# A two-block MetaFormer kernel: order of work in the outlook stage, and smaller portions of side work in attention

## The chip, the cores and the metric

The kernel runs on one core of one Trainium2 chip. The metric is the device time of one execution in microseconds (us). The core has five engines that run their own instruction streams: TensorE (PE) for matrix products, VectorE (DVE), ScalarE (ACT), GpSimd (POOL) and SyncE (SP), which here only issues DMA transfers. Engines wait for one another by semaphores. Everything is computed in fp32.

## The reference

The input x has 4 images of 32 x 32 positions (1024 tokens each) and 384 channels. Two blocks follow one another, each with a mixing part and a feed-forward part, and each part is added to its input.

```python
# block 0, mixing: attention with grouped queries
q, k, v = heads(qkv_w @ ln_c(x))                      # 12 heads of 32, N = 1024 tokens
attn = softmax(q k^T * scale)
gw = one_hot(argmax(q gp^T))                          # each query's group, 48 groups a head
q_mean = mean of the q of a group;  qmw = q_mean k^T  # (48 groups, N)
mask = the 96 largest of each row of qmw
attn = attn * row * mask.sum(groups);  attn /= attn.sum(over queries) + 1e-8
x = x + (attn v) @ proj_w^T
# block 0, feed-forward: 4 experts of width 1536, the best 2 of each token, gelu
x = x + sum_e weight_e * (gelu(ln_t(x) w1_e) w2_e)
# block 1, mixing: outlook attention, 3 x 3 windows, 12 heads
v = ln_c(x) Wv^T;  a = ln_c(x) Wa^T                   # a: 12 heads x 9 x 9 at each position
attn = softmax(a * scale, last axis)
out = attn @ (v of the 9 neighbours);  y = the 9 outputs added back onto the 9 neighbours
x = x + y @ Wo^T
# block 1, feed-forward with Kronecker weights
h = gelu(ln_t(x) kron(c_fc_1, c_fc_2)^T);  x = x + h kron(c_proj_1, c_proj_2)^T
```

## The kernel before

Tokens lie in 32 tiles of 128 (8 tiles an image). The kernel runs four stages in one program: attention (`attention`, line 159), experts (`experts`, 1547), outlook (`outlook`, 1767), and the Kronecker feed-forward (`Kron.run`, 2173). Attention and outlook are under a manual schedule: every engine's instructions stand in the order in which the Python code emits them. So an instruction that waits holds back all that its engine was given after it. The same is true of the DMA issues of SyncE.

**Attention.** The main loop takes 192 steps of some 5.7 us, 4 a head, 12 heads an image, 4 images. In a step u of head n it emits the scores of a pair of key tiles (L627, TensorE), their exponentials (L637, ScalarE), the product with v of an earlier step (L645 into ps_o) and the row sums (L645 into ps_z). In step u == 0 of the next head, `gather` copies the sums and sends them over two small DMAs (z_row L661, zz L663). In u == 1 `spread` adds them, inverts them and sends them out again (r_row L675, rz L677), so that rz holds one value a query on all partitions. `share` (L689, VectorE) multiplies the exponentials with rz, and with the mask's count. A `Head` object, when made, issues eight DMAs that copy q and k of its head into q4 and k4; it is made at u == 1 of the head before, at the very end of the step.

Beside this main work each step carries side work for other heads and images, written as Python generators that are advanced once or a few times a step: `prepare` (normalise, turn, q and k of an image), `groups` (the one-hot groups and the group means; `choose` and `tally` are its two later parts), `topk` (an iterative search for the 96th value of each row; `search` advances it twice a step), and `routed`, `Router.route`, `Router.first` and `Router.schedule` (the routing of tokens to experts, advanced once a step). `prepare` and `groups` yield a price and a condition; `prepared` takes the next portion if its condition holds, until a step's budget (PACE) is spent. `topk` and the routing yield only to end a portion. `later(f)` runs f at the beginning of the next step; `ends` holds what is emitted when the main work and the portions of a step are.

In `topk`, a VectorE chain (L377 to L407) ends with the value `between`; then comes a yield, and then the ScalarE instruction L411, which counts what lies above it. ScalarE has the next exponentials behind it.

**Outlook.** A loop over steps i = 0 to 31 and a few more. Step i makes, for tile i: the scores (`scores`, twelve matmuls ps_a L1881, with a maximum and a subtraction on VectorE, L1887 and L1888), the exponentials (`exps`, L1895, ScalarE), the normalised next tile (`norm`, xn L147), its transposition (`turn`, ps_tr L155, ScalarE copy L156), `values` (ps_v L1928) and `share`: VectorE adds up the nine exponentials of a window (L1901 to L1905, tiles a_rows and a_sum), inverts (L1906), multiplies (L1908), and SyncE issues the moves of the normalised shares by one row of the image (L1918, L1919 into up; L1920, L1922 into down; about 40 to 122 KB each).

For the tile two steps back: `outer` (two ScalarE copies, L1942 and L1943, of the moved shares into u; they stand ahead of the exponentials of tile i on ScalarE), `inner` (three VectorE additions, L1949 to L1951) and `band`: six matmuls ps_c L1960, two multiplications into co (L1968), a DMA of co into a DRAM buffer (room, L1975, 150 KB), and, when that has landed, a DMA that reads it back as a band (L1981, 1560 KB); SyncE itself waits for the landing of room before it issues the read. For the tile four steps back: `sort` (three ScalarE copies L1991 of the landed band into own) and `gather` (ps_y L2004, the product with v). Finished rows go through `mix` (ps_wo L2019) and `mixed` (added to x, L2026). `add` brings in the experts' output for later tiles (yt, L1541 and L1844).

Loads for later tiles are issued in steps 1, 2, 5 and 8; step 8 has `Kron.load`, which issues the weights of the last stage and then emits on VectorE the sums that need them (f2sum L2127, row, wide).

Of the kernel before, what the change touches and what calls it, by code (L numbers as in the profile page):

```python
# [10 lines left out]
FP = mybir.dt.float32  # L11
# [6 lines left out]
P = 128  # L18
# [140 lines left out]
def attention(net, outer, router, x, x1, unsafe, qkv_wT, gpT, proj_wT, proj_w, gate_w, gate_b):  # L159
# [24 lines left out]
    with ExitStack() as ctx:  # L184
# [161 lines left out]
        def topk(b, t):  # L346
# [61 lines left out]
            yield  # L408
            over = small("tk_over")
# [40 lines left out]
        def prepare(b):  # L450
# [22 lines left out]
            for half in range(2):  # L473
# [6 lines left out]
                for t in range(4):  # L480
                    st = tiny.tile([P, 6], FP, name="ln_st", tag="ln_st", bufs=2)
                    nc.vector.bn_stats(st, xt[:, t, :])
                    nc.vector.bn_aggr(mv[:, t, :], st)
                    if t % 2:
                        yield 0.3, None
# [45 lines left out]
        def groups(b):  # L531

            im = images[b]
            for c in range(KC):
# [28 lines left out]
                def tally(two, ones_):  # L563
                    one = NB // 2 * (KC * b + c) + two
                    nc.scalar.activation(ones_, ones_, AF.Copy, accum_out=onehot[:, one : one + 1])
                    chosen.append(two)
# [204 lines left out]
        def routed(b):  # L771
# [25 lines left out]
            if b == B - 2:  # L797
                yield
                router.first()
# [63 lines left out]
        for step in range(STEPS + OUT + 2):  # L863
# [42 lines left out]
            if u == 1 and n + 1 < NHEAD:  # L906
                heads.append(Head(n + 1))
# [307 lines left out]
class Router:  # L1215
# [71 lines left out]
    def route(self, b, logit, mean, rs):  # L1287
# [20 lines left out]
        nc.vector.tensor_tensor(prob, prob, all_(one), ALU.mult)  # L1308
        pairs = [P, NB, NE, NE]
# [3 lines left out]
        for t, op, mask in ((ge, ALU.is_ge, self.lower), (gt, ALU.is_gt, self.upper)):  # L1313
            nc.vector.tensor_tensor(t, other, mine, op)
            nc.vector.tensor_tensor(t, t, mask.unsqueeze(1).to_broadcast(pairs), ALU.mult)
        nc.vector.tensor_tensor(ge, ge, gt, ALU.add)
# [28 lines left out]
        nc.vector.tensor_tensor(at, src, base.unsqueeze(1).to_broadcast(wide), ALU.add)  # L1345

# [8 lines left out]
        nc.vector.tensor_reduce(slot[1], part, AX.X, ALU.max)  # L1355
        there = []
# [25 lines left out]
    def first(self):  # L1382
# [9 lines left out]
        nc.vector.tensor_reduce(full, fills, AX.X, ALU.add)  # L1392

# [12 lines left out]
        nc.vector.tensor_scalar(pre, pre, float(NFIRST), float(UNITS), ALU.min, ALU.mult)  # L1406
        self.firsts = self.rows(self.pool, "first", NFIRST, 1)
# [359 lines left out]
def outlook(net, wv, wa, wo, left, router, kron, loads):  # L1767
# [15 lines left out]
    with ExitStack() as ctx:  # L1783
# [113 lines left out]
        def share(i):  # L1897
            b, t = place(i)
# [4 lines left out]
            sm = work.tile([P, 2, PW], FP, name="a_sum", tag="a_sum")  # L1903
            nc.vector.tensor_tensor(sm, rows[:, :, 0, :], rows[:, :, 1, :], ALU.add)
            nc.vector.tensor_tensor(sm, sm, rows[:, :, 2, :], ALU.add)  # L1905
            nc.vector.reciprocal(sm, sm)  # L1906
# [132 lines left out]
        for step in range(last + 1):  # L2039
# [5 lines left out]
            if 0 <= i - 2 < NT:  # L2045
                outer(i - 2)
            if i < NT:
                scores(i, 0)
                scores(i, 1)
                exps(i)  # L2050
            if 0 <= i - 2 < NT:
                inner(i - 2)
            if i + 1 < NT:
                xn = norm(i + 1)
            done = []
            for one in mixes.pop(step, []):
                done.append(mix(*one))
                if len(done) == 2:
                    mixed(*done[0])
                    mixed(*done[1])  # L2060
                    gauged += [j for j, _ in done]
                    done = []
            if 0 <= i - LAG < NT:
                gather(i - LAG, 0 if (i - LAG) % NB < 5 else 1)
            if i + 1 < NT:
                turn(i + 1, xn)
            for one in done:
                mixed(*one)
                gauged.append(one[0])
# [3 lines left out]
            if 0 <= i - 2 < NT:  # L2073
                band(i - 2)
# [22 lines left out]
class Kron:  # L2097
# [19 lines left out]
    def load(self, fc1T, fc2, proj1T, proj2):  # L2117
# [7 lines left out]
        nc.sync.dma_start(out=p2, in_=proj2.rearrange("a b -> (a b)").partition_broadcast(P))  # L2125
        self.f2sum = const.tile([P, 1], FP, name="f2sum")
# [166 lines left out]
def metaformer_kernel(  # L2293
# [19 lines left out]
    def rest(router, done):  # L2313

        with ExitStack() as late:
# [17 lines left out]
            def weigh(queue, tile_, w):  # L2333
# [9 lines left out]
                8: lambda: kron.load(fc1T, fc2, proj1T, proj2),  # L2343
            }
# [14 lines left out]
    with tc.If(tc.nc.values_load(unsafe[0:1, 0:1], min_val=0, max_val=1) != 0):  # L2359
        with ExitStack() as outer:  # L2360
# [4 lines left out]
            with ExitStack() as inner:  # L2365
                router = routing(inner)
                for b, given in enumerate(gates(net, router.psum, gate_w, gate_b)):
                    for _ in router.route(b, *given):
                        pass
                    if b == B - 2:  # L2370
                        router.first()
# [61 lines left out]
```

## Time and profile before

| what | value |
|---|---|
| time, median of 3 runs | 2778.15 us (2777.52 to 2788.7) |
| profiled execution | 2777.38 us, its span 2774.9 us |
| TensorE busy | 2565.5 us, 92% of the span, mean granted clock 0.959 |

The stages, in us of the span (with the busy time of TensorE, VectorE and ScalarE in each window):

| stage | window | length | PE | DVE | ACT | granted clock |
|---|---|---|---|---|---|---|
| loading, first preparing | 0 to 80 | 80 | 54.32 | 14.27 | 30.01 | 1.00 |
| attention | 80 to 1208 | 1128 | 1015.31 | 810.85 | 818.97 | 0.93 |
| experts | 1208 to 2251 | 1043 | 1029.13 | 532.03 | 202.48 | 1.00 |
| outlook | 2251 to 2686 | 435 | 388.88 | 346.24 | 197.64 | 0.95 |
| Kronecker feed-forward | 2686 to 2775 | 89 | 77.81 | 24.90 | 52.76 | 0.89 |

The scores of the outlook steps 0 to 31 start at 2251.45, 2260.84, 2270.12, 2282.46, 2295.0, 2305.85, 2316.71, 2328.42, 2343.71, 2371.64, 2383.57, 2395.25, 2408.52, 2419.85, 2431.52, 2443.19, 2454.51, 2466.89, 2478.76, 2490.44, 2503.72, 2515.04, 2526.71, 2538.38, 2549.71, 2563.80, 2575.66, 2587.34, 2600.61, 2611.93, 2623.60 and 2635.28 us.

How to read the lines further down: in a timeline, the start in us, the duration, the engine (SPq is SyncE's DMA issues), the line and operation, output <- inputs, and in brackets how long the engine sat idle before and what released it. In a table of waits: who waited, at which line, for whom; us in total, how many times, the longest. The granted clock is the share of full speed that TensorE was given.

### The profile page before, as it was taken

To read this page: it belongs to the slowest core of one execution; us is meant where nothing else is said; L and a number is where in the kernel's file an instruction comes from. 1 tells how busy PE (TensorE), PEld (TensorE's weight loads), DVE (VectorE), ACT (ScalarE), POOL (GpSimd) and SP (SyncE) were. 2 spreads that over 40 slices of the span, in tenths; PEclk is the share of its full clock that TensorE was granted. 3 is DMA by queue.
4 is the path that set the end of the run, shared out by engine and by line. 5 is a ranking of instruction groups with operands and counts; after the bars stand their busy time and mean duration, and the time that the engine had idled before them with its cause. 6 is when DMAs were issued, how large, how long until landed. Compare 5 with 4: busy or idle time off the path is not lost. (4 is left out here: it accounts for less than half of the span.)

```text
span 2774.9 us, 40133 instructions
## 1 busy us (share of the span) xinstructions
PE 2565.5 (92%) x14667; PEld 1558.3 (56%) x14667; DVE 1728.3 (62%) x4362; ACT 1301.9 (47%) x2119; POOL 417.8 (15%) x501
## 2 busy tenths in 40 slices
PE   6889999999999998789999999999999987999988
PEld 3323333333333332247889999999999953555532
DVE  1367778677778787647444544465455556887962
ACT  3778777677778777412221221121121123455455
POOL 1000000030003001413211112222222101110000
PEclk9989999999999998889999999999999999999989
DMA  5133434322322232454665545655655447565532
GB/s 108 33 103 92 108 86 126 95 60 63 96 73 64 59 107 69 133 175 160 230 238 207 202 170 216 232 194 217 237 205 211 175 145 221 165 201 175 173 110 93
DMA packets 215806, 404.13 MB, mean 146 GB/s; under 512 B 83344, under 2 KB 176848, under 8 KB 202544
## 3 DMA queue, kind: packets, MB, share of 16 engines
q1 hardware_dynamic: 184496, 187.82, 22.6%
q0 software_dynamic: 26960, 209.05, 22.0%
q10 hardware_dynamic: 4144, 4.61, 0.5%
q8 instruction: 118, 1.93, 0.3%
q14 instruction: 88, 0.72, 0.1%
HBM read 304.34 MB, written 49.00 MB: 127 GB/s over the span
## 5 line engine op out<-in xcount | busy, mean ns | idle before, releaser
L1702 ACT ACTIVATE h<-ps_h,up 128x256 f32<-128x256 f32 (+1 forms) x420 | 195.1, 465 | 825.3 <-PE ps_h L1697 823.7
L1697 PE MATMUL ps_h<-xbT,up 128*128 128x256 f32 (+1 forms) x2520 | 531.1, 371 | 2.5 <-ACT h L1702 1.8
L689 DVE CUSTOM_DVE_ANT_0 e<-e,rz,inv 128x1024 f32<-128x1024 f32 x384 | 475.3, 1274 | 47.3 <-DMA rz<-r_row 47.3
L1697 PEld LDWEIGHTS ps_h<-xbT,up 128*128 128x128 f32 x2520 | 462.6, 191 | 64.6 <-ACT h L1702 2.6
L637 ACT ACTIVATE e<-ps_s,ten 128x1024 f32<-128x1024 f32 x384 | 408.0, 1109 | 66.6 <-PE ps_s L627 40.1
L627 PE MATMUL ps_s<-q,k 32*128 32x512 f32 x1536 | 297.4, 671 | 51.5 <-ACT e L637 35.0
L645 PE MATMUL ps_o<-e,wv 128*32 128x512 f32 x1536 | 227.2, 666 | 40.3 <-DVE wv L696 38.8
L716 POOL DMA_DIRECT2D q<-po x96 | 76.2, 886 | 947.6 <-DMA q<-po 452.9
L645 PE MATMUL ps_z<-e,rt_ones 128*32 128x512 f32 x1536 | 217.1, 639 | 0.0
L373 ACT ACTIVATE below<-tk_left,tk_bound 128x1024 bf16<-128x1024 f32 (+1 forms) x160 | 184.4, 1152 | 52.4 <-DVE tk_bound L379 41.4
L1741 PE MATMUL ps_y<-wsum,hsum 128*128 128x192 f32 x1116 | 196.0, 329 | 9.5 <-DVE hsum L1657 5.2
L627 PEld LDWEIGHTS ps_s<-q,k 32*128 32x128 f32 x1536 | 92.8, 191 | 189.1 <-ACT e L637 92.0
L1741 PEld LDWEIGHTS ps_y<-wsum,hsum 128*128 128x128 f32 x1116 | 182.5, 191 | 13.2 <-DVE hsum L1657 6.6
L1881 PE MATMUL ps_a<-wa,xnT 128*128 128x486 f32 x384 | 162.1, 571 | 0.6 <-ACT xnT L156 0.6
L1745 DVE TENSOR_TENSOR y<-ps_y,y 128x192 f32<-128x192 f32 x155 | 55.5, 358 | 165.5 <-PE ps_y L1741 162.4
L645 PEld LDWEIGHTS ps_o<-e,wv 128*32 128x32 f32 x1536 | 31.5, 112 | 201.0 <-issue 66.1
L288 PE MATMUL ps_t<-xnT,wqkv 128*128 128x512 f32 x288 | 134.6, 607 | 2.4 <-ACT xnT L470 1.7
L1541 POOL DMA_INDIRECT yt<-yg,index x64 | 78.1, 1220 | 375.5 <-DVE x L1844 181.4
L645 PEld LDWEIGHTS ps_z<-e,rt_ones 128*32 128x32 f32 x1536 | 52.2, 117 | 132.0 <-issue 128.8
L1741 PE MATMUL ps_y<-down,h 128*128 128x192 f32 x744 | 126.0, 326 | 0.0
L1741 PEld LDWEIGHTS ps_y<-down,h 128*128 128x128 f32 x744 | 122.6, 190 | 1.6
L1991 ACT COPY own<-band 128x1040 f32<-128x1040 f32 x96 | 101.7, 1125 | 33.2 <-DMA band<-room 30.8
(398 smaller groups left out, 3576.7 us busy)
## 6 DMA issues: line engine op xcount, KB each, us to landing
band<-room SPq DMA_DIRECT2D x32, 1560.0 KB
rz<-r_row SPq DMA_DIRECT2D x48, 512.0 KB
yg<-y SPq DMA_DIRECT2D x67, 192.0 KB
q<-q SPq DMA_DIRECT2D x192, 64.0 KB
k<-k SPq DMA_DIRECT2D x192, 64.0 KB
room<-none SPq DMA_DIRECT2D x64, 192.0 KB
x<-x SPq DMA_DIRECT2D x35, 192.0 KB
o<-in_x_dram SPq DMA_DIRECT2D x33, 192.0 KB
```

The lines of the kernel that those rows point to most:

```text
L288: nc.tensor.matmul(ps, lhsT=lhsT(k), rhs=rhs(k), start=k == 0, stop=k == KC - 1)
L373: nc.scalar.activation(junk[:n], left[:n], AF.Sign, bias=bound[:n], accum_out=over[:n])
L627: nc.tensor.matmul(ps[:, half * 512 : half * 512 + 512], lhsT=self.k4[r, u * P : (u + 1) * P], rhs=self.q4[r, :], start=True, stop=True,)
L637: nc.scalar.activation(e, ps, AF.Exp, bias=shift, scale=QK_SCALE)
L645: nc.tensor.matmul(ps[r : r + 32, :], lhsT=lhsT(odd), rhs=self.es[2 * u + odd][:, half * 512 : half * 512 + 512], start=u == 0, stop=u == ...
L689: nc.vector.tensor_tensor_reduce(self.es[m], self.es[m], self.rz, 1.0, self.im["inv"][:, m, self.h : self.h + 1], ALU.mult, ALU.add, self. ...
L1541: self.nc.gpsimd.indirect_dma_start(out=y, out_offset=None, in_=self.net.yg[: first_row(self.complete(i // NB)), :], in_offset=bass.Indire ...
L1697: nc.tensor.matmul(ps, lhsT=up[:, o : o + P], rhs=xbT[:, k, :size], start=k == 0, stop=k == KC - 1,)
L1702: nc.scalar.activation(hs[f // 3][:, f % 3, :size], ps, AF.Gelu, bias=up[:, KC * HID + f : KC * HID + f + 1])
L1741: nc.tensor.matmul(ps, lhsT=left[f], rhs=right[:, f, :], start=f == 0, stop=f == HF - 1)
L1881: nc.tensor.matmul(pa[:, :HW_], lhsT=xnTs[i][:, k, :], rhs=wa[:, k, hh * HW_ : (hh + 1) * HW_], start=k == 0, stop=k == KC - 1,)
L1991: nc.scalar.copy(own[:, pairs], m.rearrange("p t (n h) -> p n t h", h=2)[:, pairs])
```

## The change

No arithmetic changes. In the outlook loop, `norm` of the next tile is emitted ahead of the scores. `share` is cut in two: `total` (the sums of the window) and the rest. `mixed`, then `total`, then `band` of the tile two back are emitted before `gather`, `turn`, `values` and the rest of `share`; before, `band` came after them. `Kron.load` keeps its loads at step 8, and its VectorE part moves into `Kron.fold` at step 14.

In attention, `topk` gets one more yield between the VectorE chain and L411. `prepare` for images after the first spaces its statistics by a step. `tally` marks a portion as chosen one step later, which the condition in `groups` waits for. `Router.route`, `first` and `schedule` get more yields. A `Head` is made at u == 0 of the head before, if its q and k are ready, and at u == 1 as before if not.

```diff
@@ -406,6 +406,7 @@
             nc.vector.scalar_tensor_tensor(between[:n], last[:n], -(1 - 2.0**-23), none[:n], ALU.mult, ALU.subtract)
             nc.vector.tensor_scalar(own[:n], hsel[:n, t, :], none[:n], 2.0, ALU.mult, ALU.mult)
             yield
+            yield
             over = small("tk_over")
             sign = left.bitcast(BF)[:, :NTOK]
             nc.scalar.activation(sign[:n], left[:n], AF.Sign, bias=between[:n], accum_out=over[:n])
@@ -482,7 +483,7 @@
                     nc.vector.bn_stats(st, xt[:, t, :])
                     nc.vector.bn_aggr(mv[:, t, :], st)
                     if t % 2:
-                        yield 0.3, None
+                        yield 0.3, after(1) if b else None
                 std = im["std"][:, 4 * half : 4 * half + 4]
                 nc.scalar.activation(std, mv[:, :, 1], AF.Sqrt, bias=net.eps["c"])
                 yield 0.3, after(1) if b else None
@@ -563,7 +564,7 @@
                 def tally(two, ones_):
                     one = NB // 2 * (KC * b + c) + two
                     nc.scalar.activation(ones_, ones_, AF.Copy, accum_out=onehot[:, one : one + 1])
-                    chosen.append(two)
+                    later(lambda: chosen.append(two))
 
                 for two in range(NB // 2):
                     yield 0.7, lambda: not ends
@@ -796,7 +797,7 @@
             yield from router.route(b, logit, im["mv"][:, :, 0], rs)
             if b == B - 2:
                 yield
-                router.first()
+                yield from router.first()
             if b == B - 1:
                 yield
                 yield from router.schedule(late[0])
@@ -903,7 +904,7 @@
             search()
             end()
             search()
-            if u == 1 and n + 1 < NHEAD:
+            if u < 2 and len(heads) == n + 1 < NHEAD and (u or ((n + 1) // NH, (n + 1) % NH // 4, "qk") in reached):
                 heads.append(Head(n + 1))
         residue(B - 1, 0)
         assert not ends and not others
@@ -1306,6 +1307,7 @@
         nc.vector.tensor_reduce(one, prob, AX.X, ALU.add)
         nc.vector.reciprocal(one, one)
         nc.vector.tensor_tensor(prob, prob, all_(one), ALU.mult)
+        yield
         pairs = [P, NB, NE, NE]
         ge, gt = self.temp("ge", pairs), self.temp("gt", pairs)
         other = prob.unsqueeze(2).to_broadcast(pairs)
@@ -1313,6 +1315,7 @@
         for t, op, mask in ((ge, ALU.is_ge, self.lower), (gt, ALU.is_gt, self.upper)):
             nc.vector.tensor_tensor(t, other, mine, op)
             nc.vector.tensor_tensor(t, t, mask.unsqueeze(1).to_broadcast(pairs), ALU.mult)
+        yield
         nc.vector.tensor_tensor(ge, ge, gt, ALU.add)
         sel, at = self.sel[:, tiles, :], self.at[:, tiles, :]
         nc.vector.tensor_reduce(sel, ge, AX.X, ALU.add)
@@ -1343,6 +1346,7 @@
         nc.vector.tensor_tensor(self.upto[:, b + 1, :], self.upto[:, b, :], pc[:, NE : 2 * NE], ALU.add)
         nc.vector.tensor_tensor(base, base, self.region, ALU.add)
         nc.vector.tensor_tensor(at, src, base.unsqueeze(1).to_broadcast(wide), ALU.add)
+        yield
 
         part = self.temp("part", wide)
         big = float(2 * NE * NT * P)
@@ -1353,6 +1357,7 @@
         nc.vector.tensor_scalar(slot[0], slot[0], -1.0, big, ALU.mult, ALU.add)
         nc.vector.tensor_tensor(part, at, sel, ALU.mult)
         nc.vector.tensor_reduce(slot[1], part, AX.X, ALU.max)
+        yield
         there = []
         for n in range(2):
             i = self.temp(f"there_{n}", [P, NB], mybir.dt.int32)
@@ -1390,6 +1395,7 @@
             fills, full.unsqueeze(2).to_broadcast(shape), self.steps.unsqueeze(1).to_broadcast(shape), ALU.is_ge
         )
         nc.vector.tensor_reduce(full, fills, AX.X, ALU.add)
+        yield
 
         self.start = self.pool.tile([P, B + 2, NE], FP, name="rt_start")
         self.begun = self.pool.tile([P, B + 2, NE], FP, name="rt_begun")
@@ -1404,6 +1410,7 @@
         nc.vector.tensor_tensor(taken, taken, full, ALU.min)
         nc.vector.tensor_scalar(taken, taken, float(UNITS), None, ALU.mult)
         nc.vector.tensor_scalar(pre, pre, float(NFIRST), float(UNITS), ALU.min, ALU.mult)
+        yield
         self.firsts = self.rows(self.pool, "first", NFIRST, 1)
 
     def rows(self, pool, name, n, groups):
@@ -1894,15 +1901,20 @@
             flat = attn[i].rearrange("p y s x e -> p (y s x e)")
             nc.scalar.activation(flat, flat, AF.Exp, scale=QK_SCALE)
 
-        def share(i):
-            b, t = place(i)
+        sums = {}
+
+        def total(i):
             a = attn[i]
             rows = work.tile([P, 2, 3, PW], FP, name="a_rows", tag="a_rows", bufs=1)
             nc.vector.tensor_tensor(rows, a[:, 0], a[:, 1], ALU.add)
             nc.vector.tensor_tensor(rows, rows, a[:, 2], ALU.add)
-            sm = work.tile([P, 2, PW], FP, name="a_sum", tag="a_sum")
+            sm = sums[i] = work.tile([P, 2, PW], FP, name="a_sum", tag="a_sum")
             nc.vector.tensor_tensor(sm, rows[:, :, 0, :], rows[:, :, 1, :], ALU.add)
             nc.vector.tensor_tensor(sm, sm, rows[:, :, 2, :], ALU.add)
+
+        def share(i):
+            b, t = place(i)
+            a, sm = attn[i], sums.pop(i)
             nc.vector.reciprocal(sm, sm)
             for qi in (0, 2, 1):
                 nc.vector.tensor_tensor(
@@ -2044,14 +2056,14 @@
                 sort(i - LAG)
             if 0 <= i - 2 < NT:
                 outer(i - 2)
+            if i + 1 < NT:
+                xn = norm(i + 1)
             if i < NT:
                 scores(i, 0)
                 scores(i, 1)
                 exps(i)
             if 0 <= i - 2 < NT:
                 inner(i - 2)
-            if i + 1 < NT:
-                xn = norm(i + 1)
             done = []
             for one in mixes.pop(step, []):
                 done.append(mix(*one))
@@ -2060,18 +2072,20 @@
                     mixed(*done[1])
                     gauged += [j for j, _ in done]
                     done = []
+            for one in done:
+                mixed(*one)
+                gauged.append(one[0])
+            if i < NT:
+                total(i)
+            if 0 <= i - 2 < NT:
+                band(i - 2)
             if 0 <= i - LAG < NT:
                 gather(i - LAG, 0 if (i - LAG) % NB < 5 else 1)
             if i + 1 < NT:
                 turn(i + 1, xn)
-            for one in done:
-                mixed(*one)
-                gauged.append(one[0])
             if i < NT:
                 values(i)
                 share(i)
-            if 0 <= i - 2 < NT:
-                band(i - 2)
             if 0 <= i - LAG < NT and (i - LAG) % NB == 4:
                 gather(i - LAG - 1, 1)
                 gather(i - LAG, 1)
@@ -2123,6 +2137,10 @@
         nc.sync.dma_start(out=self.wp, in_=proj1T.rearrange("(f p) a -> p f a", p=P))
         nc.sync.dma_start(out=self.f2, in_=fc2.rearrange("a b -> (a b)").partition_broadcast(P))
         nc.sync.dma_start(out=p2, in_=proj2.rearrange("a b -> (a b)").partition_broadcast(P))
+
+    def fold(self):
+        nc, A, K = self.nc, self.A, self.K
+        const, p2 = self.const, self.p2
         self.f2sum = const.tile([P, 1], FP, name="f2sum")
         nc.vector.tensor_reduce(self.f2sum, self.f2, AX.X, ALU.add)
 
@@ -2341,6 +2359,7 @@
                 2: lambda: fetch(2),
                 5: lambda: fetch(3),
                 8: lambda: kron.load(fc1T, fc2, proj1T, proj2),
+                14: kron.fold,
             }
             eng = mybir.EngineType
             with tc.manual_schedule(engines={eng.PE, eng.DVE, eng.Activation, eng.SP, eng.Pool}):
@@ -2368,7 +2387,8 @@
                     for _ in router.route(b, *given):
                         pass
                     if b == B - 2:
-                        router.first()
+                        for _ in router.first():
+                            pass
                 done = experts(net, router, x1, x2, wup, wdown, router.schedule)
         rest(router, done)
 
```

## Prediction

> **What bounds the kernel now.** I read the page's busy shares first, then time by stage, then waits inside the two stages that change, then single instructions and the chain.
>
> ```profile
> span 2774.9 us, 40133 instructions
> PE 2565.5 (92%) x14667; PEld 1558.3 (56%) x14667; DVE 1728.3 (62%) x4362; ACT 1301.9 (47%) x2119; POOL 417.8 (15%) x501
> ```
>
> TensorE is busy for 92% of the span, so 209 us are all that better ordering can recover, plus what the clock loses after idle time. In the table by stage the columns are the window, its length, busy time of PE, PEld, DVE, ACT and POOL, the granted clock, DMA share and GB/s.
>
> ```profile
> 500.00:700.00 200.00, 189.74 (x1208) 67.16 (x1201) 145.30 (x433) 148.03 (x235) 32.81 (x36) 0.97 0.28 67
> 1100.00:1176.00 76.00, 56.90 (x329) 16.46 (x333) 49.58 (x144) 36.00 (x39) 34.27 (x30) 0.78 0.45 133
> 2295.00:2400.00 105.00, 81.93 (x432) 44.13 (x431) 72.48 (x168) 42.47 (x63) 15.78 (x16) 0.90 0.62 191
> 2400.00:2500.00 100.00, 97.90 (x537) 54.29 (x539) 89.24 (x211) 53.67 (x80) 13.63 (x14) 1.00 0.65 208
> ```
>
> Attention (80 to 1208 us) and the start of the outlook stage lose time in idle gaps; the outlook stage from 2400 on is bound by TensorE to 98%. Waits in attention (waiter, releaser, us in total, times, longest):
>
> ```profile
> PE ps_s L627 <- DMA k<-k: 16.2, 10, 8.7
> PE ps_t L589 <- ACT g L565: 8.8, 8, 1.4
> ACT tk_left L411 <- DVE tk_parts L406: 36.8, 15, 5.8
> DVE e L689 <- DMA rz<-r_row: 43.4, 20, 9.0
> ```
>
> And one of the gaps behind the third line, in the timeline:
>
> ```profile
> 1064.48 1.15 ACT L411 ACTIVATE tk_left<-tk_left,tk_parts 128x1024 bf16<-128x1024 f32 x1 [1.17 <-DVE tk_parts L406]
> 1069.33 3.08 PE L627 MATMUL ps_s<-q,k 32*128 32x512 f32 x8 [4.66 <-ACT e L637]
> ```
>
> L411 stands on ScalarE ahead of the exponentials but needs a VectorE chain emitted in the same half-step. The exponentials come late and TensorE waits 4.66 us. Its eight matmuls then take 3.08 us; such a group took 1.1 us elsewhere, so a gap is paid for twice. Waits in outlook, same columns:
>
> ```profile
> PE ps_tr L155 <- DVE xn L147: 32.6, 10, 14.9
> ACT own L1991 <- DMA band<-room: 30.8, 14, 6.9
> DVE f2sum L2127 <- DMA f<-in_fc_dram: 13.0, 1, 13.0
> ```
>
> Last, lines that tell what the new order will meet. In most steps the moves of a tile are issued some 5 us after a band read, in step 6 only 2.1 us after it (SyncE's timeline). The second fence is from the chain: issue, then time to landing.
>
> ```profile
> 2326.42 0.34 SPq L1981 DMA_DIRECT2D band<-room  x1
> 2328.54 0.54 SPq L1918 DMA_DIRECT2D up<-attn  x1
> ```
> ```profile
> 2328.54 6.69 DMA up<-attn
> 2658.73 6.65 DMA band<-room
> 2666.38 6.20 DMA band<-room
> ```
>
> The 40 KB move waited until the 1560 KB read was through: 6.69 us, where a room write of 150 KB on the same queue, with nothing ahead of it, landed after 2.54 us (chain, 2344.59).
>
> **The change, part by part.** No instruction is added or removed; only the order and the half-step change. So everything is paid or gained in waits.
>
> *Outlook, fold (step 8 to 14).* f2sum stands on VectorE behind a load issued in the same step, and waits 12.96 us; xn, and with it TensorE, wait behind it. Step 8 took 27.9 us (2343.71 to 2371.64 between score starts), the like steps 16 and 24 12.4 and 14.1. Gain 27.9 − 13.2 = 14.7. The loads stay at step 8, 70 us ahead of step 14, so nothing is late next.
>
> *Norm ahead.* ps_tr waited 1.93 us for xn in steps 0 and 1. With xn ahead of the scores, the turn is then bound by the mean of the tile's chain; 0.7 of each is recovered, gain 1.4. Later steps have a ps_wo before the turn, and gain nothing.
>
> *Band ahead of gather, turn, values and share.* Two effects. (a) ps_c needs u, which ends 2.1 us after the scores; the single ps_wo ahead of it lasts 1.94. Worth 0.2 to 0.3 a step, and contained in (b). (b) SyncE now issues room, waits for its landing, issues the band read, and only then the moves (L1918 to L1922), which before stood ahead of room. All go through SyncE's one queue, so every tile's moves land behind a 1560 KB read, as in step 6. ScalarE's copies u of the next step wait for them, and queued behind those copies are the exponentials of the next tile (L1895), and behind these, on VectorE, the new total and co. co starts the next room write. That closes a loop from one step to the next:
>
> u copy 0.28 + exponential 1.02 + four instructions of total 1.68 + co 0.6 + room write to band issue 2.54 (chain) + read 6.2 (the chain's lower value) + the moves' own data, 162 KB at 250 GB/s, 0.65 = 12.97 us, call it 13.0. Where gathers of yt run beside it (steps up to 17), room to band took 2.9 to 3.05 and reads 6.7: 13.9 us. TensorE's own step is 11.3 to 11.7. The loop is open once in 8 steps: the first tile of an image issues no L1918. I give that step 11.9.
>
> Steps 3 to 7: 5 × 13.9 = 69.5 against 61.25 (2282.46 to 2343.71): +8.25. Steps 9 to 16: 7 × 13.9 + 11.9 = 109.2 against 95.25: +14. Steps 17 to 30: 13 × 13.0 + 11.9 = 180.9 against 168.4: +12.5. The last tiles' moves come behind a read as well, bounds 0 and 6, I take 2.5. With −14.7 and −1.4: outlook +21 us. Lower bound, moves not held at all: −20 (the fold, the norm, and the last band reads some 4 us earlier). Upper bound, 8.8 us from band issue to landing as in step 6 (2326.42 to 2335.23) in place of 6.85 in half the steps: +26 more.
>
> The page "DMA: Bandwidth & Descriptors" of the Trainium skill (section "Queues, rings and completion order") says that SyncE owns one ring on each of the 16 DMA engines and that descriptors are consumed there in ring order. It speaks against the change, and by it alone the outlook would lose as reckoned. Its rule to issue a DMA early and wait late ("Rules for kernel authors") would favour the earlier read, and by that rule the outlook would gain 20 us; the row of step 6 decides between them.
>
> *Attention, the extra yield before L411.* It puts L411 half a step behind its chain. The TensorE gaps next to it (2.22, 2.72, 3.26, 1.0, 2.6, 0.88, 1.67, 0.7, 4.66, 3.02) sum to 22.7 us. Three quarters go: −17. A quarter stays, as other half-steps are as full.
>
> *tally one step later.* ps_t (L589) no longer follows the last g copy of the same step: 8.8 us, −8.
>
> *Smaller chunks in preparing, route, first and schedule.* Gaps at 459, 538, 820, 1103 and 1136 us, 3.66 + 2.62 + 1.64 + 4.58 + 4.10 = 16.6, follow such VectorE bursts; the work remains, so I take 0.4: −6.5. For the last image, route and schedule need 27 calls where 23 sufficed and 30 stand before the experts; so nothing is late, and it would cost about 5.7 us (a step) a call beyond that.
>
> *Head one step earlier.* ps_s waited 16.2 us for k; the last, 8.7, is half due to rz anyway. −7. Its eight DMA issues (0.64 each, 5.2 us of SyncE) now stand between zz and r_row of the head before. r_row was issued some 2.1 us after zz, so rz becomes up to 3.6 us later. VectorE already waits 43.4 us for rz, so about half of the 48 heads have no slack there. 28 heads, 65 us of VectorE delay in all, less the slack of ps_o behind (2.4 us median): 15 us of TensorE. Bounds 0 and 65.
>
> *Clock.* Cold matmuls in attention cost about 40 us beyond their warm times; I give 0.3 back, −12, and charge 4 for the new gaps.
>
> The skill's "TensorE: Matmul & The Clock Gate" (Part 1) puts the gate's window at about 3.4 us of idleness; the trace has half-speed matmuls after 2.72 us (at 314.46). By the page's rule only the two gaps above that length, 4.66 and 4.58, and 3.66 and 4.10 would bring clock back, some 10 us.
>
> Attention: −17 − 8 − 6.5 − 7 − 12 + 15 + 4 = −31.5. Experts (790 us between 1410 and 2200 with PE 787 busy) and the last stage do not change.
>
> Sum: 2777.4 (the profiled execution; the median shown is 2778.15, 0.8 more) − 31.5 + 21 = 2766.9; 2767.
>
> **The rivals.** *Moves not held back* (packets of the small moves overtake): outlook −20 and attention −31.5 give 2726. For it: in most steps of before no wait on a move shows. Against it: step 6.
>
> *Rz becomes the bound (slower).* SyncE's issues of Head delay r_row in every head, VectorE falls behind, and its delay is passed on whole instead of 15 of 65. From 26 us of it on, attention's gain no longer covers the outlook's loss. At 50 us and 2 more of clock: 2777.4 − 50.5 + 54 + 21 = 2802. For it: L689 waits for rz in 20 cases already. Against: the head's own use of rz starts several steps later, and part of the wait is VectorE's spare time.
>
> *The yields only shift the waits.* ScalarE's and VectorE's work is the same (148 of 200 us each), and each exponential meets the next burst instead. Attention −10, outlook +21: 2788. For it: the gaps fall in many places with different releasers. Against: L411's wait has one cause.
>
> **How the numbers follow.** Chances: both mechanisms as reckoned 0.40 (its own range 2748 to 2784); moves not held 0.16; rz the bound 0.32; shifted waits 0.12. Half a per cent is 14 us, about what a measurement can tell from no change: below 2764 faster, above 2792 slower. The first case gives 0.18 faster, 0.16 same, 0.06 slower; the second 0.16 faster; the third 0.05 same, 0.27 slower; the fourth 0.02, 0.06, 0.04. Sums: 0.36, 0.27, 0.37. The range, 2724 to 2808, leaves out the far half of the second case and a third of the third.
>
> **What would show it.** Right: outlook from 2251 to 2686 becomes about 456 us long; its score starts lie 13 to 14 us apart in seven of eight steps; the granted clock there stays near 1; ScalarE's u (L1943 of before) shows waits for up<-attn in some 25 steps, 1.5 us or more each; f2sum has no wait; L411 waits for nothing; ps_s waits for k no longer. Wrong: score starts 11.5 apart with u copies that wait for nothing; or waits of L689 for rz far above 43 us with attention as long as before. The prediction fails most easily in attention, where each removed gap can give its time to the next late engine.

## The result

The changed kernel takes 2846.61 us (median; 2844.18 to 2854.02) beside 2780.45 us of the kernel before: ratio 1.0238, 95% interval 1.0207 to 1.0268. It is slower by 66 us, above the top of the predicted range. The profiled execution has a span of 2842.3 us where before had 2774.9, 67.4 more. Stages are counted here from the first matmul of their kind to the first of the next: attention from the first scores (ps_s) to the first expert matmul (ps_h), experts from there to the outlook's first scores (ps_a), outlook from there to the last stage's first ps_h.

| us | before | after | difference |
|---|---|---|---|
| attention | 1128.3 | 1147.0 | +18.7 |
| experts | 1043.0 | 1051.2 | +8.2 |
| outlook | 434.7 | 475.7 | +41.0 |
| last stage and the start | 168.9 | 168.4 | −0.5 |

The page of the changed kernel, first its busy shares, then its windows by these stages (columns: window, length, busy time of PE, PEld, DVE, ACT and POOL, clock, DMA share, GB/s):

```profile
span 2842.3 us, 40120 instructions
PE 2570.1 (90%) x14667; PEld 1560.9 (55%) x14667; DVE 1727.6 (61%) x4362; ACT 1301.2 (46%) x2119; POOL 416.7 (15%) x501
```
```profile
80.00:1227.00 1147.00, 1001.95 (x6477) 343.81 (x6477) 810.46 (x2368) 819.29 (x1239) 139.61 (x156) 0.93 0.33 84
1227.00:2278.00 1051.00, 1033.15 (x5494) 943.85 (x5494) 532.12 (x1078) 202.86 (x429) 234.71 (x233) 0.99 0.56 205
2278.00:2754.00 476.00, 402.96 (x2021) 217.93 (x2025) 346.38 (x815) 196.21 (x291) 33.07 (x36) 0.94 0.53 166
```

The work is the same by these counts (14667 matmuls, 4362 VectorE and 2119 ScalarE instructions), and TensorE is busy for 4.6 us more; the other 63 us are idle time. The waits of attention up to its last scores (waiter, releaser, us in total, times, longest):

```profile
DVE e L690 <- DMA rz<-r_row: 118.7, 36, 7.6
PE ps_o L646 <- DVE tk_parts L377: 30.9, 16, 4.7
PE ps_o L646 <- DVE wv L697: 30.0, 13, 6.1
```

The last two of them in the kernel before:

```profile
PE ps_o L645 <- DVE wv L696: 25.1, 14, 4.6
PE ps_o L645 <- DVE tk_parts L377: 1.4, 1, 1.4
```

The waits that the change was to remove are gone: ps_s no longer waits for k (16.2 us before), and L412, L411 of before, waits 2.7 us for its chain instead of 36.8. In their place VectorE waits 118.7 us for rz, where it waited 43.4, and TensorE's ps_o waits for VectorE. From the first to the last scores of attention the idle gaps of TensorE of 0.4 us and more sum to 117 us, before to 93: the gain was given back there, and more. Up to the last scores attention is thus 7.7 us longer; the other 11.1 of the 18.7 us lie between the last scores and the first expert matmul. In the outlook:

```profile
ACT u L1955 <- DMA up<-attn: 95.2, 23, 8.6
PE ps_c L1972 <- DVE u L1963: 66.5, 29, 8.9
```

u (L1943 of before) waited 5.1 us in all for that move before. The chain (start, duration, what; pieces of at most 0.04 us are left out at the dots) shows the loop of the prediction, one turn of it:

```profile
2434.32 8.70 DMA up<-attn
2443.04 0.28 ACT u L1955
2443.32 0.92 ACT attn L1902
2444.27 0.51 DVE a_rows L1909
2444.80 0.51 DVE a_rows L1910
2445.33 0.28 DVE a_sum L1912
2445.64 0.27 DVE a_sum L1913
2445.91 0.45 DVE co L1980 x2
2446.38 2.47 DMA room<-co
...
2448.91 0.33 SPq L1993
...
2449.33 8.40 DMA up<-attn
```

From one issue of the moves to the next 15.0 us pass (2434.32 to 2449.33), 8.7 of them until the move has landed behind the band read, which SyncE issued at 2433.90. In the trace's DMA packets the read's last one ends at 2441.57 us and the moves' last one at 2443.37. In the turns from 2434 to 2499 us no piece of the chain is a scores matmul. TensorE's own time grew too: it is busy for 402.96 us of the outlook, where it was busy for 388.88, with a granted clock of 0.94 after 0.95.

### The profile page after: what moved, and what is told of

Its sections match the earlier page's. It is cut to its first block, busy times and chain, and to the rows that moved or that the text cites. A ratio compares the mean times of both kernels' runs of the same rounds, so it can differ in the third digit from the quotient of the medians.

```text
span 2842.3 us, 40120 instructions
## 1 busy us (share of the span) xinstructions
PE 2570.1 (90%) x14667; PEld 1560.9 (55%) x14667; DVE 1727.6 (61%) x4362; ACT 1301.2 (46%) x2119; POOL 416.7 (15%) x501
## 5 line engine op out<-in xcount | busy, mean ns | idle before, releaser
L690 DVE CUSTOM_DVE_ANT_0 e<-e,rz,inv 128x1024 f32<-128x1024 f32 x384 | 475.8, 1276 | 132.7 <-DMA rz<-r_row 132.5
L1704 PEld LDWEIGHTS ps_h<-xbT,up 128*128 128x128 f32 x2520 | 463.1, 191 | 64.8 <-ACT h L1709 2.6
L628 PE MATMUL ps_s<-q,k 32*128 32x512 f32 x1536 | 274.0, 656 | 24.2 <-ACT e L638 24.0
L628 PEld LDWEIGHTS ps_s<-q,k 32*128 32x128 f32 x1536 | 82.3, 186 | 156.8 <-ACT e L638 87.1
L1888 PEld LDWEIGHTS ps_a<-wa,xnT 128*128 128x128 f32 x384 | 72.3, 190 | 81.0 <-issue 70.7
```

Source lines behind the costliest of these rows:

```text
L628: nc.tensor.matmul(ps[:, half * 512 : half * 512 + 512], lhsT=self.k4[r, u * P : (u + 1) * P], rhs=self.q4[r, :], start=True, stop=True,)
L690: nc.vector.tensor_tensor_reduce(self.es[m], self.es[m], self.rz, 1.0, self.im["inv"][:, m, self.h : self.h + 1], ALU.mult, ALU.add, self. ...
L1704: nc.tensor.matmul(ps, lhsT=up[:, o : o + P], rhs=xbT[:, k, :size], start=k == 0, stop=k == KC - 1,)
L1888: nc.tensor.matmul(pa[:, :HW_], lhsT=xnTs[i][:, k, :], rhs=wa[:, k, hh * HW_ : (hh + 1) * HW_], start=k == 0, stop=k == KC - 1,)
```

## The experiments

They came in four sets, each on one chip, with runs of the kernel before beside it. Before took 2777.7, 2824.6, 2785.0 and 2785.5 us in the four, so totals are compared as ratios within a set. Stage lengths (us) are those of each run's one profile, and they differ between chips and executions: the same code of attention took 1082.2, 1092.5, 1111.9 and 1090.6 us in e3, e4, e5 and e14.

| run | set | attention | experts | outlook | ratio to before, 95% interval |
|---|---|---|---|---|---|
| before, changed kernel's pair | | 1128.3 | 1043.0 | 434.7 | 1 |
| after | | 1147.0 | 1051.2 | 475.7 | 1.0238 (1.0207 to 1.0268) |
| e1_moves_first | 1 | 1152.3 | 1053.7 | 425.9 | 1.0090 (1.0066 to 1.0114) |
| e2_band_late | 1 | 1148.8 | 1052.9 | 401.4 | 0.9997 (0.9983 to 1.0012) |
| e3_head_u1 | 1 | 1082.2 | 1051.2 | 480.8 | 1.0046 (1.0026 to 1.0065) |
| e4_both | 1 | 1092.5 | 1047.0 | 428.0 | 0.9859 (0.9834 to 0.9884) |
| e5_best | 2 | 1111.9 | 1063.0 | 404.6 | 0.9752 (0.9732 to 0.9771) |
| e6_yield | 2 | 1145.2 | 1056.2 | 431.0 | 0.9942 (0.9922 to 0.9961) |
| e7_small_issues | 2 | 1207.8 | 1059.7 | 476.9 | 2917.3 us, one run |
| e8_portions | 2 | 1131.2 | 1063.2 | 431.4 | 0.9880 (0.9855 to 0.9906) |
| e9_fold | 3 | 1132.3 | 1046.4 | 419.5 | 0.9935 (0.9913 to 0.9956) |
| e10_norm | 3 | 1131.3 | 1044.4 | 418.6 | 0.9926 (0.9905 to 0.9947) |
| e11_head_early | 3 | 1182.0 | 1048.7 | 429.6 | 1.0166 (1.0145 to 1.0187) |
| e12_before_again | 3 | 1131.3 | 1045.3 | 432.3 | 2782.8 us, one run |
| e13_routing_as_before | 4 | 1096.1 | 1043.6 | 404.7 | 0.9761 (0.9738 to 0.9783) |
| e14_best_again | 4 | 1090.6 | 1055.2 | 403.7 | 0.9752 (0.9727 to 0.9776) |

**The queue or the order, in the outlook.** The first run leaves the order on TensorE, VectorE and ScalarE as changed, and only issues the band's two DMAs behind the moves (lines left out at the dots):

```diff
         def band(i):
-            t = i % NB
             u = us.pop(i)
...
-            room = net.room[t]
+            cos[i] = co
+
+        cos = {}
+
+        def land(i):
+            co, room = cos.pop(i), net.room[i % NB]
             nc.sync.dma_start(
...
                 values(i)
                 share(i)
+            if 0 <= i - 2 < NT:
+                land(i - 2)
```

> The changed kernel, but in the outlook the two DMAs of the band (room write, band read) are issued behind the four moves of the step; TensorE, VectorE and ScalarE keep the order of the changed kernel. Queue theory (the moves stand behind a 1560 KB read on SyncE's queue): the score starts go back to 11.3 to 12 us, u no longer waits for up<-attn (95 us before), outlook (first scores to the last stage) 476 -> 412 to 420 us, total 2847 -> about 2787. Order theory (ps_c and co ahead of gather, turn and values cost the time themselves): outlook stays above 460 us, total above 2830.

The second puts all of `band` behind `share`, as before.

```diff
-            if 0 <= i - 2 < NT:
-                band(i - 2)
             if 0 <= i - LAG < NT:
                 gather(i - LAG, 0 if (i - LAG) % NB < 5 else 1)
...
                 values(i)
                 share(i)
+            if 0 <= i - 2 < NT:
+                band(i - 2)
```

> The changed kernel, with the whole band of the tile two back (matmuls, co and both DMAs) behind share again, as before; norm ahead, total apart and the fold at step 14 stay. Both theories of the outlook expect 412 to 420 us and about 2787 in total; by the queue theory it equals the run in which only the DMAs go back, by the order theory it is at least 40 us faster than that.

The outlook takes 475.7 us as changed, 425.9 with the moves first, 401.4 with the band late. So what stands ahead of the moves at SyncE costs about 50 us, and both theories hold in part: the order alone costs another 24.5 us, which the loop had hidden. The first run undoes two things at once, the read's data ahead of the moves and SyncE's wait for the landing of room, and no run separates them. In the turn shown the shares are multiplied from 2447.12 to 2448.43 us and the first move goes out at 2449.33, so the wait for room held it for 1 to 2 us there, and the landing behind the read took the 8.4 us that follow. Waits of the run with the moves first:

```profile
ACT u L1955 <- DMA up<-attn: 6.6, 2, 5.1
PE ps_c L1971 <- DVE u L1963: 29.2, 28, 4.6
```

The first line is the queue theory's (95.2 us are now 6.6). The second is the price of the order: ps_c stands on TensorE ahead of gather, turn and values and waits for u in 28 steps. With the band late that wait is 1.8 us. The chain of the run with the moves first goes from the scores over VectorE to ps_c (pieces under 0.4 us are not listed):

```profile
2452.83 4.90 PE ps_a L1888 x12
2457.76 0.68 DVE a_max L1894
2458.49 0.55 issue
2459.92 1.15 PE ps_c L1971 x6
```

Such a step takes 12.2 us, 11.7 with the band late. Between these scores and ps_c TensorE is not idle for long: it runs a ps_wo from 2457.56 to 2459.66 us and then stands still for 0.26 us. Steps 2 to 8, 16 and 24 have no ps_wo ahead of ps_c, and there it stands still for 2.2 us each time (before ps_c at 2320.53, 2331.03 and 2342.86, for example). Steps 2 and 3 are 2.2 and 2.3 us longer than with the band late. Steps 5, 6 and 8 are 3.9 to 4.1 us longer, and there the granted clock falls as well: it is 1.00 from 2286 to 2330 us and 0.90 from 2330 to 2400, 0.76 from 2342 to 2349.

**The early Head.** One line is put back:

```diff
-            if u < 2 and len(heads) == n + 1 < NHEAD and (u or ((n + 1) // NH, (n + 1) % NH // 4, "qk") in reached):
+            if u == 1 and n + 1 < NHEAD:
                 heads.append(Head(n + 1))
```

> The changed kernel, with a Head made at u == 1 alone, as before. Theory that Head's eight DMA issues delay r_row and rz: VectorE's waits for rz fall from 132 to below 60 us, first scores of attention to first expert matmul 1147 -> about 1090 us (38 below before's 1128, since the other parts gain), total about 2790. Rival, that the smaller portions themselves cost it: rz falls too, but attention stays above 1135 us and the total above 2834.

Attention falls from 1147.0 to 1082.2 us, and VectorE's wait for rz to 29.4, from 132.5 over the whole of attention:

```profile
DVE e L690 <- DMA rz<-r_row: 29.4, 19, 4.4
```

With both causes undone (the moves first, Head at u == 1):

> The changed kernel with the moves first and with Head at u == 1. If both causes are as said, the two gains add: about 2730, 50 us below before. If one of them is not the cause, 2780 or above.

The ratio is 0.9859, 37 us below before's 2777.7; I had expected 50, since the order's 24.5 us were not in the sum. The two gains add: from the changed kernel's ratio of 1.0238 the single runs take 0.0148 and 0.0192, the run with both 0.0379. The rest of the change is thus above all a gain in attention, 1128.3 to between 1082 and 1093 us.

The Head alone on the kernel before is the same edit the other way:

> The kernel before with a Head made at u == 0 alone. Predicted 15 us of delayed rz less 7 us of k, within bounds of 0 and 65. From the changed kernel and the one with Head at u == 1 on the first chip the price should be about 60 us (2.1%), with VectorE's waits for rz above 100 us; if it costs less than 25 us here, the smaller portions make the early Head dear (they shift VectorE's work to where rz is used).

Its attention is 1182.0 us beside 1131.3 of the kernel before in the same set: +50.7 us, with 143.5 us of waits for rz. So it is dear by itself. In the company of the smaller portions it costs 60 and 67 us on one chip (1152.3 beside 1092.5, 1148.8 beside 1082.2). By these figures the portions add 9 to 16 us to it, no more than the same attention differs by from one execution to another.

To tell SyncE's issue time from the data in its queue, eight tiny DMAs take the place that the early Head had:

```diff
+            if u == 0 and 0 < n and n + 1 < NHEAD:
+                for r in range(8):
+                    tiny_ = tiny.tile([32, 2], FP, name=f"none{r}", tag=f"none{r}", bufs=1)
+                    nc.sync.dma_start(out=tiny_, in_=ten[:32, :2])
             if u == 1 and n + 1 < NHEAD:
                 heads.append(Head(n + 1))
```

> The changed kernel with Head at u == 1, and eight added DMAs of 256 bytes each at u == 0, where the early Head had its eight of 64 KB (the added copies are used by nothing). If SyncE's issue time between zz and r_row is what delays rz: waits for rz go back from 29 to above 100 us and attention to first expert matmul from 1082 to above 1130. If it is the 512 KB that stand in the queue ahead of r_row: waits for rz below 60, attention below 1100.

VectorE's wait for rz is 111.5 us, and attention takes 1207.8 us, 96 more than the same attention without them in this set (e5_best, 1111.9). SyncE's timeline in this run, and below it in the run with Head at u == 1 alone:

```profile
311.29 0.37 SPq L664 DMA_DIRECT2D zz<-z_row  x1
...
312.33 5.05 SPq L910 DMA_DIRECT2D none<-ten  x8
...
318.11 0.56 SPq L676 DMA_DIRECT2D r_row<-rr  x1
```
```profile
296.72 0.38 SPq L664 DMA_DIRECT2D zz<-z_row  x1
...
298.88 0.33 SPq L676 DMA_DIRECT2D r_row<-rr  x1
```

Eight issues of next to no data take SyncE 5.05 us, and r_row goes out 6.8 us after zz instead of 2.2. Over 48 heads the median is 6.6 us here, 6.9 in the changed kernel, 2.8 in before and 3.4 with Head at u == 1. So the issue time alone brings the delay, and the bytes are not needed for it; from r_row to rz the median is 1.9 us with the tiny DMAs as with the early Head's. Why the tiny ones cost 96 us, more than the Head's own 60 to 67, stays open: this is one execution, and the Head's eight issues still follow at u == 1.

**The pieces of attention that gain.** The yield before L411 alone on the kernel before:

> The kernel before with the one yield before L411 alone. My prediction gave it 17 us of gaps and part of 12 us of clock: attention to first expert matmul 1128 -> 1100 to 1108, total about 2753. Rival (the wait moves to the next late instruction): within 5 us of before.

The tally and the smaller portions alone:

> The kernel before with tally one step later and the smaller portions of prepare, route, first and schedule alone. Predicted 14.5 us of gaps and some clock: attention to first expert matmul 1128 -> 1108 to 1115, total about 2760. Rival: the work only shifts, within 5 us of before; by it the yield before L411 has all of the 46 us that attention gained.

0.58% and 1.20% faster (0.39 to 0.78 and 0.94 to 1.47), 16 and 34 us of 2824.6. So both theories that the work only shifts are refuted. The yield gave less than the 24 us reckoned, the smaller portions and the tally about twice their 18. This set has no profile of the kernel before, so where in the kernel these us lie isn't shown. Together they are 50 us; in the first set attention without the early Head gained 46 and 36.

**The pieces of the outlook that gain.** The fold alone:

> The kernel before with the VectorE part of the last stage's preparation at step 14 alone. Predicted 14.7 us: step 8 of the outlook 28 -> 12 to 14 us, the rest of the steps as before, total 0.5% faster. If the wait on the load only moves (to the loads of step 8 in SyncE's queue), step 8 stays above 20 us and the total within 5 us of before.

Step 8 takes 14.2 us where the kernel before in the same set took 30.4; no wait of f2sum is left. The norm alone:

> The kernel before with the norm of the next tile ahead of the scores alone. Predicted 1.4 us. The run with band behind share had steps 0 to 3 of 8.0, 8.1, 8.3, 8.3 us instead of 9.4, 9.3, 12.3, 12.5; if the norm alone does this, the outlook is 10 us shorter here, and steps 16 and 24 stay at 12.5; if the earlier total and mixed have a part in it, 2 to 4 us.

The outlook is 418.6 us beside 432.3. Steps 0 to 3 take 8.0, 8.1, 8.3 and 8.3 us beside 9.4, 11.0, 10.9 and 10.8, and steps 16 and 24, which like the first ones have no ps_wo before the turn, take 10.3 and 10.4 beside 14.1 and 12.5. The norm alone does it, and even in later steps; step 8, where VectorE still waits for f2sum's load, falls from 30.4 to 24.4 us. Some of it goes back in step 4 (17.3 beside 10.9 us) and step 7 (16.0 beside 12.3). The kernel before again, for these stage lengths:

> The kernel before, unchanged, for its stage lengths on the chip of this set: attention to first expert matmul about 1128, outlook about 435 us if the chip is like the first.

**The version without both losses**, with all gains kept:

> The changed kernel with the whole band behind share and with Head at u == 1; kept are the norm ahead, total apart, the fold at step 14, the yield before L411, tally one step later and the smaller portions. If the gains of the two runs that undid one each add up: outlook 401 us, attention to first expert matmul about 1083 to 1092, total about 2777 - 33 - 41 = 2703. If they share a cause, 2740 or more.

Ratio 0.9752 (0.9732 to 0.9771): 71 us below before's 2824.6, where 74 were expected, so the gains add. It beats both kernels.

**The end of attention.** One difference stayed open: from the last scores of attention to the first expert matmul the kernel before takes 33.2 us, the changed one 44.3, and with Head at u == 1 it is 47.2. So all of the routing's new yields were taken back in the best version (six, in `route` and `first`; `schedule` itself has none new; and `yield from router.first()` back to the plain call), with the best version beside it:

> The version with band behind share and Head at u == 1, with route, first and schedule in the portions of before; tally, statistics, the yield before L411 and all of the outlook stay. Theory: the six more yields make the first experts' weight gathers come only 5 to 8 us before the last scores (32 to 42 us in the kernel before), and they fill the DMA engines just when the last head's sums travel; undone, last scores to first expert matmul 44 to 47 -> 34 to 36 us, and the total about 10 us shorter, unless the bigger VectorE portions cost as much in the steps before. Rival: the tail is long because VectorE itself is late; then it stays at 44 to 47.

> The version with band behind share and Head at u == 1, again, beside the run in which the routing's portions go back: last scores to first expert matmul 44 to 47 us, ratio to before about 0.975.

The theory of the tail holds: 34.8 us against 47.6. But the ratios are 0.9761 and 0.9752, no difference. The table of windows says why; the first line is of the best version, the second of the one with the routing as before:

```profile
1120.00:1134.00 14.00, 5.83 (x44) 1.72 (x36) 1.36 (x4) 4.66 (x5) 5.38 (x6) 0.82 0.95 362
```
```profile
1115.00:1126.00 11.00, 1.83 (x16) 0.32 (x16) 1.09 (x1) 1.63 (x3) 4.15 (x6) 0.75 0.85 302
```

In both, there is a stretch of some 11 to 14 us in which the DMA engines are nearly full (0.95 and 0.85, 362 and 302 GB/s) and TensorE is busy for only 5.83 and 1.83 us: at its start GpSimd gathers the first experts' weights. With the smaller portions their issues come 5 to 8 us ahead of the last scores (at 1118.3 and 1120.5 us) and hold up the last head's sums: VectorE waits 12.8 us for zz to land, and then TensorE 11.8 us for wv. With the routing as before they come 29 to 42 us ahead of the last scores (at 1099.5 and 1112.4 us) and hold up the last head's k instead:

```profile
PE ps_s L628 <- DMA k<-k: 9.7, 2, 9.5
```

The kernel before has the same wait, 8.7 us, at the same place. So the portions do not make the stall, they move it. The other sums cancel as well: the portions save 18 us until the last scores (1043.0 beside 1061.3), 13 of it goes in the tail and 11.6 in the experts (1055.2 beside 1043.6).

## Why the prediction was wrong

The direction was wrong (2767 forecast; 2846.6), and the forecast range ended at 2808. By its own steps:

- *Fold, −14.7:* right. Step 8 fell from 27.9 to 14.4 us in the changed kernel, and the fold alone took 12.8 us off the outlook.
- *Norm ahead, −1.4:* the first term that was mis-sized, on the other side. It is worth 13.7 us alone, since it reaches the steps that have no ps_wo (0 to 8, 16 and 24), not only steps 0 and 1. Fold, norm and the earlier total and mixed together leave 401.4 of 434.7 us once the band is out of their way, −33 where I had 16; fold and norm alone make up 26.5 of it.
- *Band ahead, the loop, +37:* the mechanism was right, the size was not. The steps 3 to 7 took 72.9 us (69.5 reckoned), 9 to 16 115.8 (109.2), 17 to 30 191.1 (180.9), and the last one 55.0 against 51.0 (+4, reckoned 2.5). Beside the run with the band late, band ahead cost 74 us (475.7 against 401.4), twice the 37; 50 of it is what stood ahead of the moves and 24.5 the order. In the loop the term that failed is "read and the moves' own data, 6.85", counted from the read's issue: in the chain's turns 6.8 to 8.7 us passed from the moves' issue, which comes 0.4 us after the read's, to their landing. I had worked the lower bound into the sum, and the row of step 6 that I showed as evidence, 6.69 from an issue 2.1 us after the read's, already said 8.8 from the read's issue. I kept that for the range. Also, the moves of before stood mostly 6 to 7 us behind a read, not "some 5", and the 14 us by which TensorE's busy time grew were in no term.
- *Effect (a), "contained in (b)":* true in the changed kernel, where u came late for another reason. Alone it costs 24.5 us (moves first against band late). In a step with a ps_wo TensorE's wait is 0.26 us, as reckoned, and the step 0.5 us longer; what the term left out are the steps without a ps_wo, 2.2 to 4.1 us in most of them.
- *Yield, tally, portions and clock in attention, −43.5:* about right in sum; attention without the early Head gained 46.1 us in one run and 35.8 in another. Its parts were not: the yield is worth 16 us in total, the tally and the portions 34. The rival that they only shift the waits is refuted for the total of this part.
- *Head one step earlier, −7 + 15 + 4 = +12:* the step that turned the sign. Alone it costs 50.7 us, in the changed kernel 64.8. I had both bounds (0 and 65) and the mechanism, counted 65 us of VectorE delay, and then let ps_o's slack absorb 50 of them. It absorbed little: ps_o's waits for VectorE grew (tk_parts from 1.4 to 30.9 us, wv from 25.1 to 30.0). The true value lies near the upper bound. This is the rival "rz becomes the bound", which I had priced at 2802 with 50 us (its sum leaves out the 2 us of clock that it names). What it lacked was the outlook's other 20 us, the experts' 8 and 15 more in attention. The prediction's own sign of being wrong showed: L690 waits 118.7 us for rz, far above 43, and attention is no shorter.
- *Experts, 0, and "nothing is late":* the experts are 8.2 us slower. No wait for the schedule shows, but the first experts' weights were gathered 6 to 8 us ahead of the last scores instead of 32 to 42, and 11 us more passed between the last scores and the first expert matmul (47.6 us with the routing's new yields and 34.8 without, in one set). They lengthened the experts' stage as well: 1055.2 us with them, 1043.6 without in the same set. One wait that grew is TensorE's for hsum, whose longest went from 4.2 to 8.3 us; where the other 4 us come from stays open.

Where the sum went: −31.5 + 21 + 0 = −10.5 was forecast; 18.7 + 41.0 + 8.2 − 0.5 = 67.4 was measured. Of the 78 us between, about 53 are the Head, 20 the outlook (37 more for the band ahead, less 17 that fold, norm and the rest of its order gave beyond the sum), 8 the experts, less 3 that the rest of attention gained beyond the sum.

The page "DMA: Bandwidth & Descriptors" of the Trainium skill ("Queues, rings and completion order") was on the right side: moves issued behind the read on the same queue landed behind it, 8.4 us after their issue in the turn shown. Its rule to issue a DMA early ("Rules for kernel authors") says nothing of what else the early issue pushes back; both losses here are early issues.

## What to carry to other kernels

Moving a DMA issue forward has a price for everything that it passes on the issuing engine and in its queue. Look for what stands behind it in that queue, and ask whether that sits in a loop: eight issues of 0.6 us cost 50 us because a small transfer that each head waits for stood behind them, and a 1560 KB read, with SyncE's wait ahead of it, cost 50 us because moves that the next step waits for stood behind it.

When a delay is on an engine with thin slack, take the bound of full propagation for the sum and the absorbed part for the range, not the other way round. And where the same stretch is limited by two things, price each by itself: the order's 24.5 us did not show while the loop was the limit, and fold, norm and the rest of the outlook's order gave their 33 us only without it.

## What the runs showed of the hardware that was not expected

Eight DMAs of 256 bytes took SyncE 5.05 us to issue, as long as eight of 64 KB (the early Head's, 302.28 to 307.51 us in the changed kernel, 5.2). While GpSimd's gather of the experts' weights kept the DMA engines busy (share 1.02 and 0.88 in the windows 1180 to 1185 and 1185 to 1190 us), a 4 KB r_row took 10.2 us from its issue to the next instruction that needed its landing, in the changed kernel:

```profile
1178.36 0.32 SPq L676 DMA_DIRECT2D r_row<-rr  x1
1188.54 0.32 SPq L678 DMA_DIRECT2D rz<-r_row  x1
```

In the same place of the kernel before, 1.4 us passed (1171.54 to 1172.95). And chips differ: the same best version took 2753.3 us on one and 2718.1 on another, but 0.9752 of the kernel before on both.
